# Early gate projections, early products with D, the first states' transfers on ScalarE's queue, and another PSUM room for the value product, in a one-core AdaLN layer

## The chip, the cores and the metric

One core of a Trainium2 chip runs the whole program in one launch. The metric is the device time in microseconds (us) of one execution. TensorE is PE in the views, VectorE is DVE, ScalarE is ACT, GpSimd is POOL and SyncE, which here only issues DMAs, is SP.

## The reference

```python
h = layernorm(x) * (1 + ca) + sa               # x: 4 batches, 2048 tokens, 512 columns, f32
x = x + ga * attn(h)
h = layernorm(x) * (1 + cb) + sb
x = x + gb * ffn(h)

attn(u):   omega = clip(softplus(u W_omega^T + b)); zeta = sigmoid(u W_zeta^T + b); F = u W_B^T + b_B
           A = omega^2; S = 1/(1 + DT^2 A); d = 1 - zeta      # 64 oscillators, states z and y
           z, y = d (S z - DT A S y), d (DT S z + S y)        # a scan over the 2048 tokens
           z, y = z + F[:64], y + F[64:]
           return [z y] C^T + u D_mat^T
ffn(x):    x_prev = x shifted by one token
           r = sigmoid((mu_r x + (1 - mu_r) x_prev) W_r^T)
           k = (mu_k x + (1 - mu_k) x_prev) W_k^T
           return r * (relu(k)^2 W_v^T)
```

sa, ca, ga, sb, cb and gb are six rows for each batch, made from a small input by one product with `wmod`; ga and gb are kept at least 0.25 away from zero.

## The kernel before

The tokens are cut into 8 blocks of 256, and each block has 4 batches, so there are 32 units; unit i is block s = i // 4, batch b = i % 4. Each unit passes through two classes. `gts[i]` (a gate unit) makes the inputs of the scan: `project` multiplies the transposed, not yet normalized x (`xt`, loaded transposed from DRAM) with a weight that holds (1 + ca) already (`wgb`, L233); `norm` finds the layernorm's factors on ScalarE (L185, L191) and POOL (L195 to L197); `send` writes these factors as rows to DRAM (`st`, L201), and `spread` reads them back to all partitions (`bc`, L212); `multiply` applies them to the projection (L251), and `deliver` sorts the result into the block's `maps` with its bias (L264, L266). When all four gate units of a block are delivered, `scan(s)` runs the recurrence on VectorE: softplus and damping, 8 steps inside each of 32 chunks (L306 to L319), a tree over the chunks up and down (L335 to L353), and the states at the end (L374 to L381). `by_batch` sorts the states (ScalarE L401 for block 0, VectorE L404 for the others), and eight DMAs carry them to `y` (L407). The scan of the next block runs beside the finish units of this one: its pieces wait in a list `side`, and `take(budget)` puts as many of them into VectorE's order as the budget, in us, allows.

`fin[i]` (a finish unit) does the rest. In block 0: `attend` makes the product with D (`direct`, L463, into PSUM `pd_c`) and the product of the states with C (`states`, L486, into `pc_c`), and VectorE adds both to x (L471, L513); then come the second layernorm (`normalize`, ScalarE L573), `mix` (transposes on PE, L593; scaling and token shift in turn on ScalarE L599 and VectorE L602, the first column on POOL L605), `key` (L626, relu and square on ScalarE L630, L617), `receptance` (L738, L740) and `value` (L753, then L756, L757 and the store). The loop runs one unit ahead: in stage i it does the key of unit i, `attend` of unit i+1, the receptance of i, the `mix` of i+1, the value of i. From block 1 on key and receptance are made by another method with seven products in place of eight, and D and C go into one PSUM sum.

D_mat is different for each batch (scaled by ca and ga), so a `Turn` job for each batch makes it: `d_scaled` scales rows on VectorE (L958) with a row that PE has spread over the partitions (`scale_rows`, L122), `rows` scales with ga on ScalarE (L972), `turn` transposes on PE (L981), `keep` copies back on ScalarE (L985), and `keep_in_dram` saves it (L795), because its SBUF room `dg` serves other things later.

All instructions of an engine run in the order in which the program text issues them, DMA issues included: there is no scheduler here. POOL and ScalarE issue DMAs out of the same order as their arithmetic, so a DMA that has to wait holds what stands behind it. A DMA also waits for the one that had its completion semaphore before it (eight are used in turn by all DMAs of SP and ScalarE).

In block 0 before the change the order was: projections of units 0 to 3, scan(0) in one piece on VectorE, the six rows of wmod, D for batches 0 and 1, products with D of units 0 and 1, projections 4 and 5, then the states; D for batches 2 and 3, the products with D of units 2 and 3, and the projections 6 to 9 stood behind the states, between the stages of the loop.

Of the kernel before, what the change touches and what calls it, by code (L numbers as in the profile page):

```python
# [9 lines left out]
F32 = mybir.dt.float32  # L10
# [11 lines left out]
P = 128  # L22
# [28 lines left out]
def adaln_layer_kernel(ctx: ExitStack, tc: tile.TileContext, x, x_t, c_t, wmod, w_gate, w_b, b_gate, b_f, c_mat, d_mat,  # L51
# [76 lines left out]

    y_of = {}

    class Block:
# [15 lines left out]
    class Gates:  # L147
# [89 lines left out]
        def project_pieces(self):  # L237
            u = self.u

            def piece(i, k):  # L240
                if i == k == 0:
                    self.pg = ps1.tile([P, 2, W], F32, tag="pg", name=f"pg_{u.tag}")
                nc.tensor.matmul(  # L243
                    self.pg[:, i, :], wgb[:, u.b, k, ts(i, P)], self.xt[:, k, :], start=(k == 0), stop=(k == KC - 1)
                )

            return [lambda i=i, k=k: piece(i, k) for i in range(2) for k in range(KC)]

        def multiply(self, tag="g"):
# [18 lines left out]
    def scan(s):  # L268
# [123 lines left out]
        def by_batch(q):  # L392
# [12 lines left out]
            for r in range(2):  # L405
                for i in range(2):
                    nc.sync.dma_start(y_of[s][ts(i, M), 2 * q + r, :], t[i][ts(r, M), :])  # L407

# [16 lines left out]
    class Finish:  # L425
# [46 lines left out]

        def products(self, room=(ps3, "px")):

            self.pd = [self.direct(n, room) for n in range(NT)]

        def add_products(self):
            for n in range(NT):
                self.add_direct(n, self.pd[n])

        pd = None

# [5 lines left out]
        def attend(self, between):  # L488
# [11 lines left out]

            if self.pd is not None:
                for n in range(NT):
                    states_apart(n)
            for n in range(NT):
                if self.pd is None:
                    pd = self.direct(n, stop=not self.fast)
                    if self.fast:
                        self.states(n, pd, False)
                    else:
                        states_apart(n)  # L510
                    self.add_direct(n, pd)
                if not self.fast:
                    nc.vector.tensor_add(self.x[:, n, :], self.x[:, n, :], pcs[n])  # L513
                if n == 0:
                    self.stats(n)
                    between()
# [225 lines left out]

        def value(self, between, parts=1):

            act, xt, u = self.act, self.x, self.u
            n_col = D // parts
            for n in range(NT):
                r = self.r[n]
                for h in range(parts):
                    at = ts(h, n_col)  # L750
                    pv = ps2.tile([P, D], F32, tag="pm", name=f"pv_{self.tag}_{n}_{h}")[:, :n_col]
                    for j, k in enumerate(range(KC) if parts == 1 else (2, 3, 0, 1)):
# [137 lines left out]
    gts[3].xt = p1.tile([P, KC, W], F32, tag="act", name="xt_3")  # L890
    load_transposed(gts[3].u, gts[3].xt)
    weights_to(dn, d_mat, nc.sync)
    weights_to(dt, d_t, nc.sync)
    wm_ga = wmod_to(wvb[:, 2], 2)

# [66 lines left out]
    class Turn:  # L962


        def __init__(self, b):
            self.dst, self.b = dg[:, b], b
            self.room = (ps2, "pm") if b < 2 else (ps3, "px")

# [5 lines left out]
        def turn(self):  # L974
            self.pts = [
                pool.tile([P, D], F32, tag=tag, name=f"turn_d{self.b}_{k}")
                for k, (pool, tag) in enumerate([(ps2, "pt")] * 2 + [self.room] * 2)
            ]
# [4 lines left out]
        def keep(self):  # L983
            for k in (2, 3, 0, 1) if self.b < 2 else range(KC):
                nc.scalar.copy(self.dst[:, k, :], self.pts[k])  # L985

    c_rows = dg[:, 3]

    def c_scaled(b, n):
        nc.vector.tensor_mul(cg[:, b : b + n], cn.unsqueeze(1).broadcast_to([P, n, D]), c_rows[:, b : b + n])  # L990

# [18 lines left out]
    def shift_rows():  # L1010

        nc.sync.dma_start(col_rows.rearrange("i b d -> (i b) d"), rows3)
        nc.sync.dma_start(c_rows, col_rows[2:3].broadcast_to([P, B, D]))
        for i in range(2):
            fin[i].shift_row = fin[i].row(0)
        fin[0].gate_row = fin[0].row(1)
# [51 lines left out]
    gts[3].multiply("soft")  # L1068
    gts[3].deliver(share=1)
    pcas = [scale_rows(b) for b in range(2)]  # L1070
    side += scan(0)
    take(0.1)
    take(0.1)
    for b in range(2):
        d_scaled(b, pcas[b])
    gts[4].load()
    weights_to(wk, w_k, nc.sync)
    weights_to(wn, w_v, nc.sync)
    take(100)

    pr = rows_of(all_mod, dt, D, "mean")
    rowm = p2.tile([P, D], F32, tag="r", name="row_mean")
    nc.scalar.copy(rowm, pr)
    rowa = mod_rows(wm_ga, "ga")
    wm_sb = wmod_to(wvb[:, 2], 3)
    nc.scalar.copy(pmean, turned(rowm, "mean", 2 * B))
# [4 lines left out]
    turn_d = [Turn(b) for b in range(B)]  # L1093
    xs67 = p1.tile([P, 4, D], F32, tag="mixed", name="xs67")
    gts[4].norm()
    gts[4].send(nc.gpsimd)
    rowb = mod_rows(wm_gb, "gb", room=px)
    turn_d[0].rows()
    rowc = mod_rows(wm_cb, "cb", room=px)
    gts[5].load()  # L1100
    xt45 = wvb[:, 1].rearrange("p k d -> p (k d)").rearrange("p (i k w) -> p i k w", i=2, k=KC)
    for i in (4, 5):
        gts[i].xt = xt45[:, i - 4]
        load_transposed(gts[i].u, gts[i].xt)
    for i in (6, 7):
        gts[i].xs = [xs67[:, NT * (i - 6) + n, :] for n in range(NT)]
        load_natural(gts[i].u, xs67[:, NT * (i - 6) : NT * (i - 5), :])
    gate_cols(gb, turned(rowb, "gb"), "b")
    nc.scalar.activation(mod[:, CB], turned(rowc, "cb"), AF.Identity, bias=1.0)
    pr = ps2.tile([P, D], F32, tag="pt", name="pd0row")  # L1110
    for e in range(KC):
        nc.tensor.transpose(pr[: 3 * B, ts(e, P)], cols[:, e].rearrange("p i b -> p (i b)"), ident)
    nc.scalar.copy(rows3, pr[: 3 * B, :])
    shift_rows()
    turn_d[0].turn()
    turn_d[0].keep()
    keep_in_dram("dg", 0)
    row = mod_rows(wm_sb, "sb", room=px)
    xt67 = wvb[:, 2].rearrange("p k d -> p (k d)").rearrange("p (i k w) -> p i k w", i=2, k=KC)
    for i in (6, 7):  # L1120
        gts[i].xt = xt67[:, i - 6]
        load_transposed(gts[i].u, gts[i].xt)
    gts[4].spread(nc.gpsimd)
    turn_d[1].rows()
    nc.scalar.copy(mod[:, SB], turned(row, "sb"))
    shift_factors()
    gts[5].norm()
    gts[5].send(nc.gpsimd)
    fin[0].products()
    turn_d[1].turn()  # L1130
    turn_d[1].keep()
    keep_in_dram("dg", 1)
    gts[4].project()
    pcas = [scale_rows(b, pm) for b in range(2, B)]
    gts[5].spread(nc.gpsimd)
    fin[1].products((ps2, "pt"))
    gts[5].project(ps3.tile([P, 2, W], F32, tag="px", name="pg_5"))


    c_scaled(0, 2)  # L1140
    take(1)
    fin[0].add_products()
    fin[0].shift(nc.vector)
    fin[1].add_products()
    gts[4].multiply()
    gts[6].norm()
    gts[6].send(nc.gpsimd)
    fin[0].attend(lambda: None)
    fin[0].normalize()
    c_scaled(2, 2)  # L1150
    d_scaled(2, pcas[0])
    d_scaled(3, pcas[1])
    gts[6].project()
    fin[1].shift(nc.vector)
    weights_to(wr, w_r, nc.sync)
    gts[7].norm()
    gts[7].send(nc.gpsimd)
    gts[6].spread(nc.gpsimd)
    fin[0].mix(lambda: None)
    gts[7].project(ps3.tile([P, 2, W], F32, tag="px", name="pg_7"))  # L1160
    gts[8].load_t()
    gts[4].deliver(share=1)
    gts[5].multiply()
    gts[5].deliver(share=1)
    gts[7].spread(nc.gpsimd)
    gts[8].load()
# [5 lines left out]
    def gates(j):  # L1172
        gts[j].project()
        gts[j].multiply()
        gts[j].deliver()

    def turn(*jobs):
        for t in jobs:
            t.turn()
            t.keep()  # L1180

    def rows(*jobs):
        for t in jobs:
            t.rows()

# [6 lines left out]
    for i, f in enumerate(fin):  # L1192
        at = i % B
        ahead = fin[i + 1] if i + 1 < len(fin) else None
        if i < 4:
# [5 lines left out]
            if i == 0:  # L1201
                ahead.attend(lambda: None)
                ahead.stats(NT - 1)
                ahead.norm_factors()
            if i < 2:
                rows(turn_d[i + 2])
            if i == 0:
# [9 lines left out]
            if i == 3:  # L1217
                sums_t(receptance_weights, quarters_of(wr))
            if i:
                ahead.attend(lambda: take(2))  # L1220
                ahead.normalize()
            else:
                ahead.norm_apply()
            value_scaled(i)
            if i == 3:
                fetch("dg", i + 3)
            if i == 0:
                gts[7].multiply()
                gts[7].deliver(share=1)
                gts[8].norm_dve()  # L1230
                gts[8].send()
                gts[8].spread()
                gts[9].norm_dve()
                gts[9].send()
            if i == 1:
                gates(9)
            if i:
# [3 lines left out]
            if i == 0:  # L1241
                side += scan(1)
                take(0.1)
                take(0.1)
            gts[i + 9].load_t()
            gts[i + 9].spread()
            f.value(lambda: take(3 if i == 0 else 4))
            if i < 3:
                ahead.gate_row = ahead.row(1)
            if i < 2:  # L1250
                turn(turn_d[i + 2])
                keep_in_dram("dg", i + 2)
                gates(8 if i == 0 else 10)
        else:
# [181 lines left out]
```

## Time and profile before

| what | value |
|---|---|
| times of three runs | 1139.86, 1146.07, 1148.36 us (median 1146.07) |
| profiled execution | 1144.09 us, of which the span of the instructions is 1142.3 us |
| granted TensorE clock over the span | 0.981 of full speed |
| PE busy | 1092.9 us (96%) |
| DVE busy | 756.1 us (66%) |
| ACT busy | 646.9 us (57%) |
| POOL busy | 185.0 us (16%) |
| moved by DMA | 177.73 MB, 156 GB/s on average |
| first product with states (`pc_c`) | starts at 102.00 us |
| first product of block 1 with D (`pd_c` at L463) | starts at 244.06 us |

Times inside the profile are us from the start of the span. "Idle before" is the time for which an engine stood still ahead of an instruction, and the arrow names what ended it. A matmul in f32 is shown as two instructions, so "x16" is eight matmuls.

### The profile page before, as it was taken

Reading aid. Unit: us, or ns where it says so; the run is one execution under the profiler, and the core shown is the slowest. Engines: PE = TensorE matmul, PEld = TensorE weight load, DVE = VectorE, ACT = ScalarE, POOL = GpSimd, SP = SyncE. Lnnn points to the kernel's source line nnn. Section 1 sums busy time; section 2 is a strip of 40 time slices with the busy share of each in tenths; the row PEclk is TensorE's granted clock in tenths of the full one; section 3 lists DMA queues with packets and bytes.
Section 4 is the critical chain, followed back from the end, with each engine's and each line's share of the span. In section 5 each row is a group of like instructions: output and inputs, shape, how many; then the busy total and the mean of one; then the engine's idle time right before and its main releaser. Section 6 shows DMA issues by size and latency. Waiting matters only on the chain.

```text
span 1142.3 us, 14439 instructions
## 1 busy us (share of the span) xinstructions
PE 1092.9 (96%) x4692; PEld 732.8 (64%) x4692; DVE 756.1 (66%) x1838; ACT 646.9 (57%) x1336; POOL 185.0 (16%) x377
## 2 busy tenths in 40 slices
PE   7895898989999999999999999999999999999998
PEld 4553464556667667766666677666666665566666
DVE  5793776746876568666876568665876567664444
ACT  1651764535666576557666576557665565434443
POOL 1221211121122111111111111111121101111110
PEclk9888998999999999999999999999999999999999
DMA  9985569346056754474556854474565644444211
GB/s 312 298 138 111 143 135 202 104 126 217 24 178 191 193 162 161 141 173 130 166 178 188 187 171 127 146 200 119 178 176 170 162 139 138 148 157 138 102 56 37
DMA packets 138803, 177.73 MB, mean 156 GB/s; under 512 B 22876, under 2 KB 96860, under 8 KB 130920
## 3 DMA queue, kind: packets, MB, share of 16 engines
q1 hardware_dynamic: 135720, 175.49, 54.4%
q10 hardware_dynamic: 2688, 0.79, 0.3%
q0 software_dynamic: 320, 0.53, 0.3%
q8 instruction: 37, 0.61, 0.2%
q14 instruction: 38, 0.31, 0.1%
HBM read 147.34 MB, written 25.25 MB: 151 GB/s over the span
## 4 chain that ended last, share of the span: by engine, by line
PE 69%; DMA 14%; DVE 7%; ACT 6%; issue 1%; SPq 1%; POOL 1%; DVEq 0%; POOLq 0%; ACTq 0%
PE pv_c L753 14%; PE pd_c L531 13%; PE pxk_c L656 7%; DMA xt<-in_x_t_dram 7%; PE pxr_c L656 7%; PE pg L243 5%; PE pzk_c L656 4%; DMA bc<-st 3%; PE pzr_c L656 3%; PE pd_c L486 3%; PE pg L233 2%; PE pk_c L626 2%; PE pr_c L738 2%; PE pt_c L593 2%; PE pyk_c L656 2%; PE pyr_c L656 2%
## 5 line engine op out<-in xcount | busy, mean ns | idle before, releaser
L753 PE MATMUL pv_c<-wvb,act_c 128*128 128x512 f32 (+1 forms) x528 | 226.6, 582 | 4.5 <-ACT r_c L740 4.5
L531 PE MATMUL pd_c<-dg,xt 128*128 128x512 f32 x432 | 206.2, 593 | 0.0
L753 PEld LDWEIGHTS pv_c<-wvb,act_c 128*128 128x128 f32 x528 | 100.0, 191 | 111.4 <-issue 100.3
L602 DVE SCALAR_TENSOR_TENSOR mixed_c<-pt_c,prev_f,mixed_c 128x255 f32<-128x255 f32 x256 | 118.1, 481 | 72.3 <-ACT mixed_c L599 72.1
L599 ACT ACTIVATE mixed_c<-pt_c,mod,now_f 128x256 f32<-128x256 f32 x256 | 130.2, 559 | 25.3 <-DVE mixed_c L602 19.5
L266 ACT ACTIVATE maps<-g,bias 64x256 f32<-64x256 f32 x112 | 83.1, 742 | 73.4 <-DVE g L251 65.9
L531 PEld LDWEIGHTS pd_c<-dg,xt 128*128 128x128 f32 x432 | 74.5, 191 | 55.9 <-issue 54.3
L243 PE MATMUL pg<-xt,wgb 128*128 128x256 f32 x320 | 85.4, 379 | 0.0
L471 DVE SCALAR_TENSOR_TENSOR x<-pd_c,rs,x 128x512 f32<-128x512 f32 x64 | 47.6, 746 | 52.5 <-PE pd_c L486 49.6
L550 ACT ACTIVATE xn_c<-x 128x512 f32<-128x512 f32 x44 | 27.7, 629 | 94.0 <-DVE x L471 89.8
L656 PEld LDWEIGHTS pxk_c<-dg 128*128 128x128 f32 x448 | 58.6, 191 | 27.0 <-issue 23.9
L573 ACT ACTIVATE xn_c<-x,mean_c,var_c 128x512 f32<-128x512 f32 x64 | 48.6, 808 | 42.1 <-POOL mean_c L569 42.0
L456 POOL TENSOR_TENSOR x<-x,row 128x1024 f32<-128x1024 f32 x30 | 70.9, 2363 | 8.5 <-DMA row<-col_rows 8.5
L243 PEld LDWEIGHTS pg<-xt,wgb 128*128 128x128 f32 x320 | 59.2, 190 | 7.2
L656 PE MATMUL pxk_c<-dg 128*128 128x128 f32 x448 | 59.1, 275 | 0.7 <-ACT act_c L665 0.7
L486 PE MATMUL pd_c<-cg,y 128*128 128x512 f32 x112 | 56.3, 593 | 0.0
L656 PE MATMUL pxr_c<-wvb 128*128 128x256 f32 x208 | 53.4, 379 | 0.0
L756 DVE TENSOR_TENSOR r_c<-pv_c,r_c 128x512 f32<-128x512 f32 (+1 forms) x66 | 44.0, 667 | 9.2 <-PE pv_c L753 9.2
L605 POOL TENSOR_TENSOR mixed_c<-mixed_c,edge_c 128x4 f32<-128x4 f32 x64 | 12.8, 201 | 215.1 <-ACT mixed_c L599 200.9
L251 DVE TENSOR_TENSOR g<-pg,bc 128x512 f32<-128x512 f32 x32 | 22.0, 687 | 38.7 <-DMA bc<-st 20.2
L757 DVE TENSOR_TENSOR r_c<-r_c,x 128x512 f32<-128x512 f32 (+1 forms) x66 | 44.6, 676 | 2.3
L674 DVE TENSOR_TENSOR act_c<-act_c,pzk_c 128x256 f32<-128x256 f32 x28 | 11.7, 419 | 51.8 <-PE pzk_c L656 51.8
(245 smaller groups left out, 2023.3 us busy)
## 6 DMA issues: line engine op xcount, KB each, us to landing
dg<-dg SPq DMA_DIRECT2D x30, 1024.0 KB, 7.0
xt<-in_x_t_dram SPq DMA_DIRECT2D x116, 256.0 KB, 7.8
wvb<-wv SPq DMA_DIRECT2D x26, 1024.0 KB, 15.0
x<-in_x_dram SPq DMA_DIRECT2D x32, 512.0 KB, 7.0
out_dram<-r_c SPq DMA_DIRECT2D x62, 256.0 KB, 2.1
xs<-in_x_dram SPq DMA_DIRECT2D x54, 256.0 KB, 12.2
row<-col_rows SPq DMA_DIRECT2D x36, 256.0 KB, 16.5
wvb<-in_wmod_dram SPq DMA_DIRECT2D x5, 1024.0 KB, 8.9
```

Source lines behind the costliest of these rows:

```text
L243: nc.tensor.matmul(self.pg[:, i, :], wgb[:, u.b, k, ts(i, P)], self.xt[:, k, :], start=(k == 0), stop=(k == KC - 1))
L266: nc.scalar.activation(there, here, AF.Identity, scale=sign, bias=bias[src, i, b : b + 1])
L456: engine.tensor_tensor(xt, xt, self.shift_row.unsqueeze(1).broadcast_to([P, NT, D]), ALU.add)
L471: nc.vector.scalar_tensor_tensor(xt, pd, r, xt, ALU.mult, ALU.add)
L486: nc.tensor.matmul(pc, y_of[u.s][:, u.b, ts(n, P)], cg[:, u.b, :], start=start, stop=True)
L531: nc.tensor.matmul(pds[n], self.h[:, k, ts(n, P)], dg[:, self.at, k, :], start=(k == 0), stop=False)
L573: nc.scalar.activation(self.xn[:, n, :], self.x[:, n, :], AF.Identity, bias=self.mean[:, n : n + 1], scale=self.var[:, n : n + 1],)
L599: nc.scalar.activation(m, pt, AF.Identity, bias=mod[:, SB, k, b : b + 1], scale=now_f[:, b, i, k : k + 1])
L602: nc.vector.scalar_tensor_tensor(m[:, 1:], pt[:, : W - 1], prev_f[:, b, i, k : k + 1], m[:, 1:], ALU.mult, ALU.add)
L656: nc.tensor.matmul(to[:, j, :], left[:, k, ts(j, P)], right[:, k, :], start=start and j == k == 0, stop=(k == 1), skip_group_check=True,)
L753: nc.tensor.matmul(pv, act[:, k, ts(n, P)], wvb[:, self.at, k, at], start=(j == 0), stop=(j == KC - 1))
L757: nc.vector.tensor_add(r[:, at], r[:, at], xt[:, n, at])
```

## The change

Names and lines in the diff are those of the program text. What it does:

- The transposed x of gate units 4 to 7 is loaded early into the rooms of `dg[2]` and `dg[3]`, and their projections are made before the states. Each result is copied out of PSUM by ScalarE (`keep_raw`), to be multiplied later. Projections 8 and 9 stand directly after the first products with states, where 6 and 7 stood, and are kept in the same way.
- All four `Turn` jobs and the products with D of finish units 0 to 3 stand before the states. ScalarE scales each product by the layernorm's factor on its way out of PSUM (`products`), and VectorE adds the two tiles of a unit in one instruction (`add_products`). `d_scaled` for batches 2 and 3 stands inside scan(0), after its reciprocals and after its third chunk step.
- `by_batch` of block 0 issues the transfers of the states on ScalarE's queue.
- C's rows come in two halves, the second one after the room of the first early product is free.
- `norm` of units 8 and 9 is on ScalarE; it was `norm_dve` on VectorE. The norms of units 6 and 7 read x from `wr`, and W_r is loaded when both are done.
- `value` of units 0 to 3 takes its PSUM from the pool `px` (three rooms) in place of `pm` (two rooms, which receptance uses too).

```diff
+    raw_gates = wvb[:, 1].rearrange("p k d -> p (k d)").rearrange("p (g i w) -> p g i w", g=4, i=2)
+    made_early = [wvb[:, b // 2 * 2, ts(b % 2, NT), :] for b in range(B)]
...
+        def keep_raw(self):
+            raw = raw_gates[:, self.u.i % 4]
+            nc.scalar.copy(raw, self.pg)
+            self.pg = raw
...
-                    nc.sync.dma_start(y_of[s][ts(i, M), 2 * q + r, :], t[i][ts(r, M), :])
+                    (nc.sync if s else nc.scalar).dma_start(y_of[s][ts(i, M), 2 * q + r, :], t[i][ts(r, M), :])
...
-            self.pd = [self.direct(n, room) for n in range(NT)]
+            for n in range(NT):
+                r = rs[:, self.u.b, self.u.s, 0, n : n + 1]
+                nc.scalar.activation(made_early[self.u.b][:, n, :], self.direct(n), AF.Identity, scale=r)
         def add_products(self):
-            for n in range(NT):
-                self.add_direct(n, self.pd[n])
+            nc.vector.tensor_add(self.x, self.x, made_early[self.u.b])
...
-        def value(self, between, parts=1):
+        def value(self, between, parts=1, room=(ps2, "pm")):
...
+    rowa = mod_rows(wm_ga, "ga")
+    wm_sb = wmod_to(wvb[:, 2], 3)
+    pr = rows_of(all_mod, dt, D, "mean")
...
     for b in range(2):
         d_scaled(b, pcas[b])
+    gts[4].project()
...
+    take(6.3)
...
     rowb = mod_rows(wm_gb, "gb", room=px)
+    rowc = mod_rows(wm_cb, "cb", room=px)
+    gts[4].keep_raw()
+    gts[5].project(ps3.tile([P, 2, W], F32, tag="px", name="pg_5"))
+    gts[4].norm_means()
     turn_d[0].rows()
...
+    gts[5].keep_raw()
...
+    gts[6].project()
+    turn_d[0].turn()
+    turn_d[0].keep()
+    pca = scale_rows(2)
+    d_scaled(2, pca)
+    take(6)
+    turn_d[1].rows()
+    row = mod_rows(wm_sb, "sb", room=px)
+    gts[6].keep_raw()
...
+    gts[4].norm_squares()
+    gts[4].send(nc.gpsimd)
+    gts[7].project()
     fin[0].products()
     turn_d[1].turn()
     turn_d[1].keep()
+    gts[7].keep_raw()
+    pca = scale_rows(3)
+    d_scaled(3, pca)
+    take(100)
+    turn_d[2].rows()
...
+    fin[1].products()
+    turn_d[2].turn()
+    turn_d[2].keep()
+    gts[8].load_t()
+    gts[5].norm()
+    gts[5].send(nc.gpsimd)
+    turn_d[3].rows()
+    fin[2].products()
+    turn_d[3].turn()
+    turn_d[3].keep()
     gts[5].spread(nc.gpsimd)
+    gts[9].load_t()
+    fin[3].products()
     take(1)
+    c_scaled(0, c01)
     fin[0].add_products()
     fin[0].shift(nc.vector)
     fin[1].add_products()
+    c23 = c_rows(2, made_early[0])
     gts[4].multiply()
     gts[6].norm()
     gts[6].send(nc.gpsimd)
     fin[0].attend(lambda: None)
     fin[0].normalize()
...
+    gts[8].project()
+    gts[4].deliver(share=1)
+    gts[8].keep_raw()
     fin[1].shift(nc.vector)
+    gts[6].spread(nc.gpsimd)
+    fin[0].mix(lambda: None)
+    gts[9].project(ps3.tile([P, 2, W], F32, tag="px", name="pg_9"))
     gts[7].norm()
     gts[7].send(nc.gpsimd)
+    weights_to(wr, w_r, nc.sync)
...
             if i:
+                if not ahead.fast:
+                    ahead.add_products()
                 ahead.attend(lambda: take(2))
...
-                gts[8].norm_dve()
+                gts[8].norm()
...
-                gts[9].norm_dve()
+                gts[9].norm()
...
-            f.value(lambda: take(3 if i == 0 else 4))
+            f.value(lambda: take(3 if i == 0 else 4), room=px)
...
-            if i < 2:
-                turn(turn_d[i + 2])
-                keep_in_dram("dg", i + 2)
-                gates(8 if i == 0 else 10)
+            if i == 0:
+                gts[8].multiply()
+                gts[8].deliver()
+            if i == 1:
+                gates(10)
```

## Prediction

> **What bounds the kernel now.** I read the granted clock and the tenths first, then the busy times of three stretches, PE's order of time, the chain that ended last, and POOL's order of time.
>
> ```profile
> PE   7895898989999999999999999999999999999998
> DVE  5793776746876568666876568665876567664444
> PEclk9888998999999999999999999999999999999999
> ...
> 39.00:102.00 63.00, 44.81 (x191) 26.05 (x189) 44.28 (x102) 28.44 (x62) 14.00 (x41) 0.84 0.88 182
> 102.00:244.00 142.00, 126.84 (x432) 81.20 (x433) 97.69 (x213) 79.50 (x145) 23.31 (x40) 0.94 0.58 141
> 244.00:1142.00 898.00, 890.34 (x3930) 603.15 (x3928) 592.40 (x1455) 529.10 (x1114) 143.45 (x282) 1.00 0.51 148
> ```
>
> The columns of the last three lines are the length, then the busy us of PE, PE's weight loads, DVE, ACT and POOL, the clock, the DMA share and GB/s. From 244 us on PE is full (890 of 898), and the change does not touch that part. So the change is worth the shift of one moment: the first product with D of block 1, at 244.06 now. Before it there are two stretches. From 39 to 102 us block 0's scan sets the end; from 102 to 244 PE is 89% busy.
>
> ```profile
> 86.78 3.62 PE L233 MATMUL pg<-wvb,wgb 128*128 128x256 f32 x16
> 102.00 3.75 PE L486 MATMUL pc_c<-cg,y 128*128 128x512 f32 x4 [11.60 <-DMA y<-maps]
> ...
> 137.16 8.54 PE L753 MATMUL pv_c<-wvb,act_c 128*128 128x512 f32 x16 [2.87 <-ACT r_c L740]
> ...
> 179.19 7.13 PE L753 MATMUL pv_c<-wvb,act_c 128*128 128x512 f32 x16 [1.60 <-ACT r_c L740]
> ...
> 231.94 8.83 PE L626 MATMUL pk_c<-mixed_c,wk 128*128 128x256 f32 x32 [3.12 <-DVE r_c L756]
> ```
>
> PE stands 11.6 us for the states. A wait of about 3 us also costs the clock: the product after it takes 8.83 in place of 7.07 us, while 1.60 us costs nothing (7.13 against 7.03).
>
> ```profile
> 80.94 2.07 ACT maps L401 x4
> ...
> 85.55 2.06 SPq L795
> ...
> 88.33 13.58 DMA y<-maps
> 101.91 0.09 issue
> 102.00 3.77 PE pc_c L486 x4
> ...
> 115.74 0.82 POOL L201 DMA_DIRECT2D st<-rs  x1 [0.29 <-POOL rs L197]
> 116.57 0.56 POOL L212 DMA_DIRECT2D bc<-st  x1
> 117.12 0.20 POOL L583 COPY edge_c<-first_f 128x8 f32<-128x8 f32 x1
> 117.41 0.20 POOL L605 TENSOR_TENSOR mixed_c<-mixed_c,edge_c 128x4 f32<-128x4 f32 x1
> ...
> 127.64 0.59 POOL L212 DMA_DIRECT2D bc<-st  x1 [9.02 <-DVE mv_c L127]
> 129.18 0.72 POOL L568 TENSOR_TENSOR var_c<-var_c,neg_half 128x2 f32<-128x2 f32 x1 [0.95 <-DVE mean_c L565]
> ```
>
> The states were sorted at 83.0 and usable at 102.0: the transfers stood on SP behind a save of D, then 13.6 us in the queue. The POOL lines show a hidden wait: `bc` (L212) stands in POOL's order and reads what `st` (L201) wrote, so POOL stands until `st` has landed. The view of DMA landings gives POOL's four `st` 10.0, 13.6, 14.1 and 11.3 us, though each moves only 2 KB. What stands behind `bc` on POOL is the column that key needs (L605) and the layernorm factors (L568).
>
> **What leaves the part after the states.** Two projections (3.45 each), the D products of units 2 and 3 (6.87 each) and two turns (1.75 each): 24.1 us of PE. It comes back only where PE sets the end.
>
> **The part before the states.** I place the built program's order and waits with the durations above. PE is free of projection 3 at 39.1. It makes two row products (0.9 each), two spread rows (0.9), projection 4, columns and rows (3.7), projection 5, columns (1.9) and projection 6: 58.6. Turn 0 ends at 60.4, and the spread row for D of batch 2 at 61.3. Now ScalarE copies turn 0 (2.05), scales D 1 (2.85), copies a row and projection 6 (1.05): 66.4, and projection 7 waits for that last copy, PE idle 3.4 us, so with 1.7 us for the clock it ends at 71.5. D products 0 end at 78.4, turn 1 at 80.2. From here PE and ScalarE alternate: turn, 1.55 us until the third of four copies is out, 6.87 of products, 1.75 of turn. With 0.95 for a column product, products 1 end at 89.6, products 2 at 99.8, products 3 at 110.0. ScalarE scales the last one (0.65), sorts half of the states (two copies, 1.04), and issues two transfers (0.55 each): 112.8.
>
> DVE loses more, unseen: `d_scaled` for batch 2 stands after the reciprocals (52.9) and waits for its row until 61.3; that for batch 3 stands from 70.0 until PE's row at 81.1, and each takes 2.25. After it 22.0 us of scan remain (58.24 to 81.4 now, less 1.1 for C): the scan ends at 105.3, 24 us later, but 5 us ahead of ScalarE.
>
> On ScalarE's queue nothing stands before the transfers that has not landed: y's other blocks land in 2.0 us (median; the bounds are 1.9 and 12.1), so states at 114.8, against 102.0. I take 2.0, since the saves of D are done by then. The Trainium skill's page "DMA: Bandwidth & Descriptors", section "Issuing engines are not separate DMA queues", speaks against any gain here: DMAs of all engines run on the same 16 DMA engines, and another issuing engine saves the issue time alone. By it block 0's own 11.5 us would stand and the states come at 124.3; the row of the later blocks says that the queue's contents made the delay. Clock losses after the three waits of 1.55 us: 0 to 1.7 each, taken as 0.
>
> **After the states, T = 114.8.** Norm 6 now stands behind the transfers on ScalarE and ends at T+5; its `st` is issued at T+7. `bc` 6 and then key's first column stand behind its landing. With 11.3 us, 0.6 for `bc` and two small steps, key 0 starts at T+20 (now T+15.7; PE waits 5.5 and loses 1.8), receptance 0 ends at T+37.4. Norm 7 ends at T+19.5, `st` 7 is issued at T+22, and `bc` 7 holds POOL until T+34.5, with unit 1's factors behind it: xn 1 at T+36.2 (now T+29.3). W_r is loaded from T+19.5; a megabyte lands in 4.8 us alone (C's rows) and 14.1 loaded, and receptance 0 needs it at T+30.5: 0 to 3 us, taken as 0.
>
> Then ScalarE is the path. Gate 7 waits for `bc` 7's landing (4.0 to 6.7) and is delivered by T+43.2. Norms 8 and 9 follow (8 passes, 5.5), with 1.3 us for the fourth x tile, whose room norm 8 frees (release to use took 2.65 at 135.4); table load and sigmoids 2.4; half of mix 1 2.9. Key 1 starts at T+55.4, now T+48.7, with 24 us less on PE. Scan(1)'s functions begin after mix 1 and end at T+62.1 (now T+45.9). The value room gives back the 2.87 us wait at 137.16, but PE then waits longer for mix 1.
>
> From T+62.1 DVE is full up to unit 3's second add: scan(1) 34.5, mix 2 4.5, unit 2's adds and statistics 4.6, unit 3's adds 2.6, three output pairs 4.1, three gates 2.1, scaled W_v 2.35, key sums 2.6: 57.4, so T+119.5. Then statistics and factors 3.4, xn and transposes 2.2, value 2 with a clock loss 8.7, key 3 6.9, projection 11 3.45: T+144.2, or 259.0 against 244.06. That is 14.9 us later.
>
> Costed at nothing: norms 8 and 9 leave DVE (3.5 us) while it idles; one add for two (0.3 a unit); copies of projections 8 and 9 stand in ScalarE's gaps around key 0; C's second half lands before norm 6. Transposed x for projection 10 lands in 7.8 (median) to 17.7 us: if the latter, DVE's third gate is up to 7 us late.
>
> The profiled execution of before is 1144.09 for a span of 1142.3; the median of the runs is 2.0 above it. I add the shift to the median: 1161.0.
>
> **The rivals.** First, POOL's wait is covered (`st` lands in a few us, or the mix is late anyway): key 0 at T+16, scan(1) from T+54.2, the end at T+136.3, 251.1: 7.0 later, 1153.1. For it: `st` on a quieter queue; against: 10.0 us was the least of four. Second, the states come no sooner on ScalarE's queue: with 12.1 us T is 124.9, 25.0 later in all, 1171. For it: the save of D 3 and x for unit 9 are in flight at 104 to 110; against: nothing large is in flight at 112. Third, on the other side: PE, not ScalarE and DVE, is the bound behind the states. Its 89% there speak for it. Then the 24.1 us return in full and the value waits (2.87, 1.60, 3.12) go too: 12.8 - 24.1 - 7.6 is 18.9 us earlier, 1127. It decides if key 1 starts before about T+36. Against it: DVE's 97.7 and ScalarE's 79.5 us there stay, in an order with longer waits.
>
> **How the numbers follow.** Forecast 0.52, first rival 0.25, second 0.13, third 0.10. A change of 1% is 11.5 us, about what a measurement here tells from none. Slower by over 1%: the second rival and most of the forecast, 0.62; within 1%: most of the first and the forecast's lower edge, 0.29; faster 0.09. The forecast's own range (`st` 10.0 to 14.1, clock losses 0 to 5, x 10 late by 0 to 7) is 1154 to 1171; with the first and second rivals it is 1147 to 1174.
>
> **What would show it.** Right: `pc_c` of unit 0 at 112 to 118; DVE idle about 8 and 11 us at `d_scaled`; key 0 released by POOL's L605 form; scan(1) starting 60 us or more after `pc_c`; PE idle over 5 us before key 1. Wrong: `pc_c` before 106, or PE over 85% busy between `pc_c` and block 1.

## The result, and the profile after

The changed kernel takes 1159.4 us in the median of four runs (1158.4 to 1161.1), the kernel before 1146.6; the ratio is 1.0124 (95% interval 1.0082 to 1.0167). The prediction was 1161.0. The profiled execution of the changed kernel has a span of 1157.3 us, against 1142.3.

The kernel before does not take the same time everywhere. In the four series of runs of this case, not all on one chip, its medians were 1146.6, 1144.2, 1125.5 and 1140.1 us. So every kernel below is compared within its own series, with the kernel before or with a neighbour that ran beside it.

The tenths and the granted clock of the page after:

```profile
PE   7987867889999999999999999999999999999998
...
PEclk8999888889999999999999999999999999999999
```

PE's fourth to ninth slices are 7 8 6 7 8 8, where they were 5 8 9 8 9 8, and the clock of the fifth to ninth is 8 throughout, where it was 9 9 8 9 9. The three stretches, cut at the first product with states and at the first product of block 1 with D (length, then busy us of PE, weight loads, DVE, ACT, POOL, then clock, DMA share, GB/s):

```profile
39.00:117.25 78.25, 63.94 (x284) 39.17 (x273) 47.81 (x102) 43.61 (x83) 12.68 (x37) 0.96 0.63 191
117.25:259.80 142.55, 109.73 (x336) 68.42 (x337) 89.26 (x199) 79.07 (x155) 25.28 (x46) 0.88 0.41 109
259.80:1157.30 897.50, 889.93 (x3929) 603.32 (x3927) 592.75 (x1455) 529.22 (x1114) 144.35 (x282) 1.00 0.52 149
```

The last stretch is what it was (897.5 us, 898.2 before). It is not quite a constant: in the profiles of all runs it takes 895.0 (e6) to 901.8 us (e2), so a difference of a few us between two times need not lie ahead of block 1. The states come 15.25 us later. The stretch behind them has 17.1 us less busy time on PE (109.73 against 126.84; the work moved away was 24.1 at full clock, and what is left runs at a clock of 0.88 in place of 0.94), and yet it is as long as before (142.55, before 142.06 to the same product): PE is busy 77% of it in place of 89%. PE's order of time shows both parts:

```profile
92.73 7.13 PE L470 MATMUL pd_c<-dg,xt 128*128 128x512 f32 x16 [1.60 <-ACT dg L992]
99.70 1.91 PE L988 MATMUL turn_d<-ident,dg 128*128 128x128 f32 x16
103.21 7.13 PE L470 MATMUL pd_c<-dg,xt 128*128 128x512 f32 x16 [1.60 <-ACT dg L992]
117.25 3.75 PE L492 MATMUL pc_c<-cg,y 128*128 128x512 f32 x4 [6.91 <-DMA y<-maps]
...
132.19 7.17 PE L629 MATMUL pk_c<-mixed_c,wk 128*128 128x256 f32 x32 [1.08 <-POOL mixed_c L608]
...
168.69 9.25 PE L629 MATMUL pk_c<-mixed_c,wk 128*128 128x256 f32 x32 [6.29 <-POOL mixed_c L608]
...
185.77 9.20 PE L741 MATMUL pr_c<-wr,mixed_c 128*128 128x512 f32 x16 [6.11 <-ACT act_c L633]
...
211.24 6.69 PE L235 MATMUL pg<-xt,wgb 128*128 128x256 f32 x16 [5.65 <-DMA xt<-in_x_t_dram]
```

From projection 7 (65.74, after a wait of 3.47 us) to 110.3 PE waits at most 1.6 us per unit, each time for ScalarE's copy of a turn, and the products themselves push the states back. Behind the states the short waits of before have become waits of 4 to 6 us, and the product after each takes up to 9.25 us where it takes 7.07 at full clock. The chain of waits names what stands in them:

```profile
110.97 1.10 ACT maps L408 x2
112.07 0.08 ACTq L414
112.25 4.87 DMA y<-maps
117.25 3.77 PE pc_c L492 x4
...
137.18 12.41 DMA st<-rs
150.17 4.12 DMA bc<-st
154.38 0.70 DVE g L258
...
158.67 2.64 DMA xs<-in_x_dram
...
165.12 1.09 ACT r_c L743 x2
```

The `st` of unit 7, 2 KB, is the largest piece of that chain between the states and block 1; `bc` stands behind its landing, gate 7 behind `bc`, the norms of units 8 and 9 behind gate 7 on ScalarE (156.60 to 163.8, with 1.7 us of it for an x tile), and then the sigmoids and `mix` of unit 1. POOL's order of time shows what else stood there:

```profile
131.06 0.59 POOL L214 DMA_DIRECT2D bc<-st  x1 [6.00 <-DMA st<-rs]
131.64 0.20 POOL L586 COPY edge_c<-first_f 128x8 f32<-128x8 f32 x1
131.93 0.20 POOL L608 TENSOR_TENSOR mixed_c<-mixed_c,edge_c 128x4 f32<-128x4 f32 x1
...
150.17 0.55 POOL L214 DMA_DIRECT2D bc<-st  x1 [12.14 <-DMA st<-rs]
150.74 0.72 POOL L571 TENSOR_TENSOR var_c<-var_c,neg_half 128x2 f32<-128x2 f32 x1
```

POOL stands 6.0 and 12.1 us in the issue of `bc`, with key's first column and then the layernorm factors of unit 1 behind it.

A third moment splits the stretch behind the states: the end of the logarithm of scan(1) on ScalarE (147.84 before, 175.46 after), from which VectorE can run the next scan. It is used for all kernels below. The start of its line, before and after:

```profile
147.21 0.63 ACT L285 ACTIVATE soft<-soft 128x512 f32<-128x512 f32 x1
...
174.83 0.63 ACT L292 ACTIVATE soft<-soft 128x512 f32<-128x512 f32 x1
```

| us | states at | states to logarithm | logarithm to block 1 | block 1 at |
|---|---|---|---|---|
| before | 102.00 | 45.84 | 96.22 | 244.06 |
| after | 117.25 | 58.21 | 84.34 | 259.80 |
| change | +15.25 | +12.37 | -11.88 | +15.74 |

So 11.9 us came back behind the logarithm (e8 below tells what they seem to be), and the two earlier parts spent them and 15.7 us more.

### The profile page after: what moved, and what is told of

Its sections match the earlier page's. It is cut to its first block, busy times and chain, and to the rows that moved or that the text cites. A ratio compares the mean times of both kernels' runs of the same rounds, so it can differ in the third digit from the quotient of the medians.

```text
span 1157.3 us, 14456 instructions
## 1 busy us (share of the span) xinstructions
PE 1094.4 (95%) x4692; PEld 733.2 (63%) x4692; DVE 752.1 (65%) x1824; ACT 661.4 (57%) x1366; POOL 186.6 (16%) x379
## 4 chain that ended last, share of the span: by engine, by line
PE 72%; DMA 12%; ACT 7%; DVE 5%; SPq 2%; issue 1%; POOL 1%; ACTq 0%; DVEq 0%; POOLq 0%
PE pv_c L756 15%; PE pd_c L534 12%; PE pxk_c L659 7%; PE pxr_c L659 6%; PE pg L245 5%; DMA xt<-in_x_t_dram 4%; DMA bc<-st 4%; PE pg L235 4%; PE pzk_c L659 4%; PE pzr_c L659 3%; PE pd_c L492 3%; PE pd_c L470 3%; DMA st<-rs 2%; PE pt_c L596 2%; PE pr_c L741 2%; PE pyk_c L659 2%
## 5 line engine op out<-in xcount | busy, mean ns | idle before, releaser
L659 PEld LDWEIGHTS pxk_c<-dg 128*128 128x128 f32 x448 | 58.7, 191 | 26.1 <-issue 24.1
L478 DVE SCALAR_TENSOR_TENSOR x<-pd_c,rs,x 128x512 f32<-128x512 f32 x56 | 41.7, 745 | 48.5 <-PE pd_c L492 48.4
L741 PE MATMUL pr_c<-wr,mixed_c 128*128 128x512 f32 x96 | 44.4, 618 | 6.5 <-ACT act_c L633 6.1
L596 PE MATMUL pt_c<-ident,xn_c 128*128 128x128 f32 x256 | 36.1, 284 | 13.3 <-ACT xn_c L576 13.3
## 6 DMA issues: line engine op xcount, KB each, us to landing
xs<-in_x_dram SPq DMA_DIRECT2D x54, 256.0 KB, 12.4
```

The lines of the kernel that those rows point to most:

```text
L596: nc.tensor.transpose(pt[:, j, ts(n, P)], xn[:, n, ts(2 * g + j, P)], ident)
L659: nc.tensor.matmul(to[:, j, :], left[:, k, ts(j, P)], right[:, k, :], start=start and j == k == 0, stop=(k == 1), skip_group_check=True,)
L741: nc.tensor.matmul(pr, mixed[:, 0, k, ts(n, P)], wr[:, k, :], start=(k == 0), stop=(k == KC - 1))
```

## The experiments

Theory: the states are later because turns and D products now stand ahead of them on PE and ScalarE, and the part behind is set by POOL's stand at `bc` and by ScalarE's norms, not by PE. Rivals: VectorE's stops inside scan(0) make the states late; the queue of the transfers does; PE is the bound behind the states.

### e1: the states' queue alone, in the kernel before

```diff
-                    nc.sync.dma_start(y_of[s][ts(i, M), 2 * q + r, :], t[i][ts(r, M), :])
+                    (nc.sync if s else nc.scalar).dma_start(y_of[s][ts(i, M), 2 * q + r, :], t[i][ts(r, M), :])
```

> The kernel before, with one edit of the change alone: the eight transfers of block 0's states go on ScalarE's queue. My theory: it was SP's queue that made the states late (sorted at 83.0 us, usable at 102.0). ScalarE has nothing ahead of them, so they land 2 to 5 us after their issue, PE reaches `pc_c` straight from projection 5 at 90.5 to 92.5, and the rest, whose length hangs on its own chains, shifts by the same 10 us: 1136 us (1133 to 1140). Rival (the issuing queue is of no account, since all DMAs share the same engines): `pc_c` at 98 to 102, 1143 to 1147 us.

1137.0 us against 1144.2; ratio 0.9956 (0.9923 to 0.9988). `pc_c` starts at 91.40, as expected. The transfers land in 4.7 to 7.2 us, against 10.5 to 12.1 in the profile of before. But block 1 starts at 236.91, only 7.2 us earlier than in the profile of before. The chain of waits shows where the rest went:

```profile
78.23 16.60 DMA dg<-dg
94.85 0.47 ACTq L407
95.37 0.77 ACT xs L185 x3
```

The last issue on ScalarE waits until the save of D for batch 1, issued on SP, has landed. It is the eighth DMA of the two engines behind that save, so the kernel's rule that eight completion semaphores are used in turn by all DMAs of SP and ScalarE would make it so. Norm 6, at 82.8 before, starts at 95.4, and unit 0's factors stand behind its factors on POOL. So the edit alone is a gain in the kernel before, less than `pc_c` gained, since ScalarE now stands in its own issues.

### e2: the changed kernel with the states on SP

```diff
-                    (nc.sync if s else nc.scalar).dma_start(y_of[s][ts(i, M), 2 * q + r, :], t[i][ts(r, M), :])
+                    nc.sync.dma_start(y_of[s][ts(i, M), 2 * q + r, :], t[i][ts(r, M), :])
```

> The changed kernel with the transfers of block 0's states back on SP's queue. Ahead of them on SP stand only the save of D 3 (issued at 103.7) and the x of unit 9 (104.1 to 106.1). Theory that the contents of SP's queue decide: these are through by 112, so the states land nearly as soon and the time is that of the changed kernel, 1158 to 1161. Theory that SP's queue is slow by itself: the 13.6 us of before come back in place of 4.9, `pc_c` at about 126 and 1168 us.

1160.0 us, as expected of the first theory; the ratio to before is 1.0177 (1.0118 to 1.0236). `pc_c` is at 115.58, block 1 at 256.11; the transfers land in 1.9 to 2.0 us on SP, against 2.2 to 4.5 on ScalarE's queue. With the states this late, their queue is of no account. The changed kernel itself was not run in this series, and e2 stands for it there; that the two take the same time rests on the other series (1159.4 and 1159.3).

### e3: norms of units 8 and 9 on VectorE

```diff
-                gts[8].norm()
+                gts[8].norm_dve()
...
-                gts[9].norm()
+                gts[9].norm_dve()
```

> The changed kernel with the norms of units 8 and 9 back on VectorE. My theory (ScalarE's order is the path from gate 7 to mix 1): the 7.2 us that they take on ScalarE between gate 7 (156.6) and the sigmoid's table (163.8) go, VectorE makes them in its idle 156 to 167; key 1 and scan(1) start 6 to 7 us earlier: 1153 us (1151 to 1156). Rival (VectorE's work sets the end of the stretch): 3.5 us more on VectorE, 1159 to 1163. Rival (PE or its waits for other things): 1159.

1154.0 us, 6.0 less than e2 beside it. From the states to the logarithm it takes 50.05 us (56.80 in e2, 58.21 in the changed kernel), and from the logarithm to block 1 85.87 (83.73 in e2). ScalarE's missing work gives 6.8 us ahead of the logarithm, and behind it 2.1 are lost, where VectorE has the extra work. Key 1 no longer waits:

```profile
161.23 7.07 PE L629 MATMUL pk_c<-mixed_c,wk 128*128 128x256 f32 x32
```

Up to the logarithm ScalarE's order was the path. The 6.0 us are not all of that kind: e3 keeps the states on ScalarE's queue, they come 1.9 us later than in e2 (117.44), and block 1 starts 2.75 us earlier (253.36). In the two profiled executions the rest lies behind block 1 (897.5 against 901.8 us), where the edit changes nothing.

### e4 and e6: factors of units 6 and 7 ahead of the states

```diff
+    gts[6].norm()
+    gts[6].send(nc.gpsimd)
     gts[5].spread(nc.gpsimd)
     gts[9].load_t()
-    fin[3].products()
+    fin[3].products(gts[7].norm)
+    gts[7].send(nc.gpsimd)
...
-    gts[6].norm()
-    gts[6].send(nc.gpsimd)
...
-    gts[7].norm()
-    gts[7].send(nc.gpsimd)
     weights_to(wr, w_r, nc.sync)
```

`products` calls its argument between its two tiles.

> The changed kernel with the norms of units 6 and 7 and their `st` moved ahead of the states, into ScalarE's idle time at 103.6 and 107.6; nothing else is moved. My theory (`bc` on POOL waits for `st` and holds key's first column and unit 1's factors): key 0 starts about 2 us earlier against the states, unit 1's factors 7 to 8 us earlier (at states + 27 in place of + 34), gate 7 is delivered 9 us earlier, and norms 8 and 9, mix 1 and scan(1) follow: 1150.5 us (1147 to 1154). Rival (POOL's wait is covered by VectorE or PE): 1158 to 1160.

1166.6 us, slower by 6.6 than e2 beside it: a miss. The stretch behind the states did become shorter (136.20 us; logarithm after 52.86), but the states came at 128.69. The chain of waits, and SP's own order:

```profile
110.97 17.62 DMA y<-maps
```

```profile
109.01 0.39 SPq L822 DMA_DIRECT2D wr<-in_w_r_dram  x1
111.36 14.71 SPq L160 DMA_DIRECT2D xs<-in_x_dram  x3
```

The earlier norms had freed the room of W_r. Its load (1 MB) and three x tiles went out in the same microseconds as the states. e6 is e4 with the states on SP, so that these loads stand behind them in the same order.

> As e4_factors_early, but the states' transfers go on SP's queue, ahead of the loads of W_r and of x for units 8 and 9. In e4 these loads, freed by the earlier norms, were issued at 109.0 and 111.4, ahead of the states, and a transfer of the states took 17.6 us in place of 4.9: `pc_c` at 128.7. My theory (the early factors shorten the stretch, the collision undid it): `pc_c` at 114 to 117, the stretch behind it as long as in e4 (136.2 us), 1150 to 1154 us. Rival (the collision is not the cause, or the loads collide with `st` and the gates instead): 1159 or more.

1148.3 us, 6.1 less than e5 beside it (told next; it has the changed kernel's states and its order behind them, and differs from e6 in the queue of the states and in the scan as well). From the states to the logarithm 51.20 us (56.40 in e5), and the stretch is 132.85 long. `pc_c` only came at 118.15, since the states took 7.2 to 10.2 us to land; with W_r behind them that is not W_r. What shared the time with them there (the `st` of units 6 and 7, `bc` of unit 5, the save of D 3) was not tried apart. POOL no longer stands for a landing:

```profile
135.34 0.77 POOL L214 DMA_DIRECT2D bc<-st  x1 [1.26 <-DVE g L258]
143.47 1.15 POOL L573 TENSOR_TENSOR var_c<-var_c,neg_half 128x2 f32<-128x2 f32 x1 [7.36 <-DVE mean_c L570]
```

Unit 1's factors now start when VectorE has its statistics. That `bc` held them in the changed kernel is shown: with the factors early, the part from the states to the logarithm takes 52.86 us in e4 and 51.20 in e6, without them 56.4 to 58.2 (changed kernel, e2, e5, e9). That the loads made e4's loss is what the rows and the order say, and e6 mends most of it.

### e5: scan(0) in one piece

```diff
-    pca = scale_rows(2)
-    d_scaled(2, pca)
     take(6)
...
-    pca = scale_rows(3)
-    d_scaled(3, pca)
+    pcas = [scale_rows(b) for b in (2, 3)]
     take(100)
+    d_scaled(2, pcas[0])
+    d_scaled(3, pcas[1])
```

> The changed kernel with `d_scaled` of batches 2 and 3 (and their spread rows) moved behind the whole of scan(0), so that VectorE no longer stands 8.4 and 11.2 us inside the scan. My theory (the alternation of turns, copies and D products on PE and ScalarE sets the moment of the states, VectorE has 5 us to spare): the scan ends near 82 us in place of 103, and still `pc_c` stays at 115 to 119 and the time at 1157 to 1162 us. Rival (VectorE's two stops delay the states): `pc_c` comes 10 to 19 us earlier and the time falls to 1141 to 1150.

1154.4 us, 2.6 below the range expected; ratio to before 1.0253 (1.0218 to 1.0288) in a series in which before takes 1125.5. The changed kernel was not run beside it, so the time alone does not tell what the edit is worth; the moment of the states does. In VectorE's order of time the scan's last big addition (L384) ends at 79.65, where it ended at 103.4 in the changed kernel, and nothing follows from it:

```profile
78.42 1.23 DVE L384 TENSOR_TENSOR maps<-maps 128x1024 f32<-128x1024 f32 x1
82.29 4.49 DVE L966 SCALAR_TENSOR_TENSOR dg<-pca,wr 128x2048 f32<-128x2048 f32 x2 [2.65 <-PE pca L122]
```

```profile
118.77 3.75 PE L492 MATMUL pc_c<-cg,y 128*128 128x512 f32 x4 [6.79 <-DMA y<-maps]
```

`pc_c` starts no sooner. A scan whose last big addition ends 24 us sooner does not bring the states while their sorting stands on ScalarE behind the last D product. The rival of VectorE's stops is out.

### e7 and e8: two pieces in the kernel before

```diff
-    keep_in_dram("dg", 1)
     gts[4].project()
...
     take(1)
+    keep_in_dram("dg", 1)
```

> The kernel before, with only the save of D for batch 1 moved behind the states' eight transfers in SP's order; they stay on SP. Theory that the transfer ahead in SP's queue made the states late, and that e1 lost part of its gain because ScalarE stood in its own DMA issues until 95.4: the states land by 90 to 92, norm 6 keeps its early place on ScalarE, the whole shift of 10 to 11 us comes through: 1134 us (1132 to 1137). Rival (other transfers on the same engines, the transposed x of units 6 and 7 above all, hold the states as well): `pc_c` at 96 or later, 1138 to 1144.

1121.3 us against 1125.5; ratio 0.9957 (0.9930 to 0.9985). The gain is there, its theory is not: `pc_c` is at 98.28, in a profile in which the same place of e8, with the save still ahead, is at 99.32. The issue of the transposed x for units 6 and 7 held SP until 83.7, and the states took 5.8 to 9.7 us to land. The rival fits this profile; but the profiled execution is the slowest of its ten (1127.55), so what brought the 4.3 us is open, and in e12 below the same edit had `pc_c` at 93.29.

```diff
-            f.value(lambda: take(3 if i == 0 else 4))
+            f.value(lambda: take(3 if i == 0 else 4), room=px)
```

> The kernel before, with only the other PSUM room for the value products of units 0 to 3. The waits of 2.87 and 1.60 us ahead of two value products, and the clock lost after the first, go: value 0 at 134.3 in place of 137.2, key 1 near 147 in place of 150.7. Theory that chains on ScalarE and VectorE set the length behind the states: the gain is taken back at the next waits (x for projection 10, key 3), 1142 to 1146 us. Rival (PE is the bound there): 4 to 6 us, 1138 to 1141.

1124.2 us against 1125.5; ratio 0.9981 (0.9960 to 1.0003). The waits ahead of two value products are gone, two others of 2.5 and 2.8 us stand ahead of the turns (for VectorE's `carry`), and the time does not tell it from no change. Its profile has one more use. In its part from the logarithm to block 1 (84.47 us) PE is busy 81.08, at full clock; in the changed kernel that part is 84.34 us long with PE busy 65.03. Of e8 and of the changed kernel:

```profile
144.98:229.45 84.47, 81.08 (x286) 51.37 (x285) 64.06 (x148) 47.37 (x92) 12.36 (x19) 1.00 0.65 161
...
175.46:259.80 84.34, 65.03 (x196) 39.76 (x195) 63.56 (x146) 40.73 (x80) 11.76 (x19) 0.88 0.52 132
```

So where x comes in time, the moved PE work bought 3 us at most even there (the part is 82.54 long in e5 and 81.65 in e6, beside e8 in one series). The 96.22 us of the profile of before hold the wait for x of projection 10 (4.02), its clock loss and the wait of key 3; e12 below, with a wait of 5.85 us for that x, takes 93.14. The part from the logarithm to block 1 is 81.7 to 85.9 us in every variant of the changed kernel.

### e9 to e12: the changed kernel again, an order with the states sooner, and the pieces of before

e9 is the changed kernel itself.

> The changed kernel itself, once more, beside the kernel before on one chip. The kernel before took 1146 us with its own profile and 1125 us in the call of e5 to e8, where its transfers landed sooner; the changed kernel with an unbroken scan (e5) took 1154 there. Theory (the changed kernel's start is set by an alternation of PE and ScalarE and by ScalarE's and POOL's order behind the states, not by large transfers): `pc_c` at 116 to 119, the first product of block 1 at 256 to 260 and 1155 to 1161 us, wherever the kernel before stands. Rival (both gain alike from sooner transfers): 1137 to 1145 where the kernel before takes 1125.

1159.3 us; ratio 1.0164 (1.0127 to 1.0200) with before at 1140.1. `pc_c` at 117.56, block 1 at 256.78. In three series the changed kernel (or e2 for it) took 1159.3 to 1160.0, while the kernel before moved from 1140.1 to 1146.6. So the same change costs 12.8, 15.9 (e2) or 19.2 us, by the series. In the series where before took 1125.5 the changed kernel itself was not run, so the rival of e9 was not put to its test; e5, at 1154.4 there, speaks against it.

e10 keeps all the moved work and changes the order; the states go on SP, as in e2 (the main lines of its edit):

```diff
     take(100)
+    take(1)
+    keep_in_dram("dg", 1)
+    d_scaled(2, pcas[0])
+    d_scaled(3, pcas[1])
     turn_d[2].rows()
...
     fin[2].products()
+    fin[0].attend(lambda: None)
     turn_d[3].turn()
     turn_d[3].keep()
...
     fin[3].products()
+    gts[6].norm()
+    gts[6].send(nc.gpsimd)
+    fin[0].mix(lambda: None)
+    gts[8].project()
```

> The changed kernel with the order of one stretch changed: scan(0) is unbroken as in e5, the states are sorted and sent (on SP, ahead of the save of D for batch 1) right after it, and the first products with states stand ahead of turn 3 and the D products of unit 3; transposes of unit 0 ahead of projection 8. No work is removed. My theory (the D products that stand ahead of the states set their moment, and the stretch behind hangs on it): `pc_c` at 101 to 104 in place of 117, key 0 at 121 to 125 in place of 132, key 1 9 to 11 us earlier, and the time 8 to 11 us under that of e9. Rival (the order of PE does not matter, something behind the states sets the end): within 3 us of e9.

1151.8 us, 7.5 less than e9, half a us short of the range expected; ratio to before 1.0098 (1.0067 to 1.0128).

```profile
99.65 1.88 PE L494 MATMUL pc_c<-cg,y 128*128 128x512 f32 x4
```

`pc_c` is 17.9 us earlier and no longer waits, so the order ahead of it made the states late; what the unbroken scan and each moved product have in it was not tried apart. Key 0 is at 119.63, but key 1 at 159.68 (7.8 earlier) and the logarithm only 66.80 us after the states. POOL took the rest, as the chain of waits shows:

```profile
117.02 11.92 DMA st<-rs
...
131.72 9.93 DMA st<-rs
142.23 3.33 DMA bc<-st
```

Norm 7's factors on POOL stand behind `bc` 6, which waits for `st` 6; then `bc` 7 waits for `st` 7: two landings in a row.

e11 is e10 with e3, and with norms and `st` of units 6 and 7 on either side of turn 3:

```diff
     fin[0].attend(lambda: None)
+    gts[6].norm()
+    gts[6].send(nc.gpsimd)
     turn_d[3].turn()
...
+    gts[7].norm()
+    gts[7].send(nc.gpsimd)
     fin[3].products()
-    gts[6].norm()
-    gts[6].send(nc.gpsimd)
...
-                gts[8].norm()
+                gts[8].norm_dve()
```

> e10 with the two other cures: norms of units 8 and 9 on VectorE (e3: 5.4 us) and norms and `st` of units 6 and 7 ahead of `mix` of unit 0 (e6: about 6 us against e5). If the three lie on one path one after another, they add: 18 to 24 us under e9, 1134 to 1141 us. Rival (behind the first cure VectorE's full stretch from scan(1) on is the bound, or x for later units): 10 to 14 us under e9.

1147.1 us, 12.2 less than e9; ratio 1.0052 (1.0029 to 1.0074). The gains do not add, as the rival said. The logarithm is done at 163.20, and 84.85 us follow, but the transposed x of unit 9 now stands in PE's way:

```profile
126.57 5.42 PE L235 MATMUL pg<-xt,wgb 128*128 128x256 f32 x16 [8.19 <-DMA xt<-in_x_t_dram]
```

It took 17.57 us to land, issued with the save of D 3, W_r and three x tiles. The profiled execution is the slowest of its twelve (1151.05), so the wait may be shorter in the others.

e12 is e7 and e8 together, the kernel before with two edits.

> The kernel before with the two pieces that helped alone: the save of D for batch 1 behind the states' transfers (e7: ratio 0.9957) and the other PSUM room for value (e8: 0.9981). If they add: ratio 0.992 to 0.996 to the kernel before, 5 to 9 us. Rival (the room gives nothing once the states come sooner): 0.995 to 0.998.

1132.6 us against 1140.1; ratio 0.9927 (0.9894 to 0.9959). That fits two pieces that add (0.9957 times 0.9981 is 0.9938), but the interval also holds the upper edge of the rival's gain (0.995), so what the room adds is not shown. It is the lowest ratio of all versions, with none of the moved PE work, though its interval overlaps those of e1 and e7.

## Why the prediction was right

The direction, the size (12.8 us forecast as 14.9) and the steps held. The size is less certain than that: with the kernel before of the other series the change costs 15.9 (e2) or 19.2 us (e9), and that the forecast lies among them is in part luck, since it did not know how much the kernel before moves. Point by point, by the names of its steps (T is the start of `pc_c`):

- The part before the states. The last D product was to end at 110.0 and ends at 110.34. PE's wait for the copy of projection 6 was 3.4 and is 3.47; the stops at `d_scaled` were to be about 8 and 11 us:

```profile
60.78 2.29 DVE L966 SCALAR_TENSOR_TENSOR dg<-pca,wr 128x2048 f32<-128x2048 f32 x1 [8.35 <-PE pca L122]
...
80.66 2.29 DVE L966 SCALAR_TENSOR_TENSOR dg<-pca,wr 128x2048 f32<-128x2048 f32 x1 [11.23 <-PE pca L122]
```

 That they do not delay the states, since ScalarE was later still, e5 shows.
- T. 114.8 against 117.25. The term that was too small is the transfer: 2.0 us, taken from the other blocks, where the chain has 4.87. It lies inside the bounds given (1.9 and 12.1; the upper one was not of other blocks but of block 0's own transfers in the kernel before). The second rival, with 12.1, is out: the eight landed in 2.2 to 4.5 us.
- Key 0 was to start at T+20 and starts at T+14.9. Norm 6 ended at T+2.8, not T+5, and `st` landed in 9.3 us, not 11.3. POOL's column was its releaser, as said, with 1.1 us of wait in place of 5.5.
- The factors of unit 1 and gate 7. `xn` was to come at T+36.2 and came at T+34.5; gate 7 was to be delivered by T+43.2 and was at T+39.3, since `bc` 7 went out at T+32.9, not T+34.5, and landed in 4.1 us. (The bounds of 4.0 to 6.7 for this landing left out one of the four of before, 10.8.)
- ScalarE's path. Norms 8 and 9 with the x tile 6.8 us (7.2); key 1 at T+55.4 (T+51.4); scan(1)'s functions done at T+62.1 (T+58.2, so the mark of 60 us was missed by 2). The 4 us are gate 7's.
- VectorE's full stretch: 57.4 us to unit 3's second add (58.6), and 24.7 to block 1 (25.8). The end, 259.0, against 259.80. VectorE is full there as forecast (busy 52.6 of 58.5 us). But a second path is level with it, which the prediction had named only as a possible delay of VectorE's third gate: the chain of waits goes by the x of projection 10 (10.67 us to land, 5.65 us of wait on PE), and both reach unit 3's normalization at 237.4. Which of them sets the end was not tried apart. An excess of 2.5 us in T, a shortfall of 3.9 behind it and 2.3 us more at the end nearly cancel; that the end is right to a microsecond is luck.
- The first rival (POOL's wait is covered) is refuted by e4 and e6, whose part up to the logarithm is 3.5 to 7 us shorter with the factors early. The third (PE is the bound behind the states) is refuted by the windows above (PE is at 77%) and by key 1 at T+51.4, where it needed T+36; e3 also gains without touching PE's work.

On the rule of the Trainium skill's page "DMA: Bandwidth & Descriptors", section "Issuing engines are not separate DMA queues", the runs are divided. For it: e2, where the queue makes no difference, and e4, where a transfer of ScalarE's queue took 17.6 us beside loads issued on SP. It allows for a gain in issue time alone, and calls that usually small. In the kernel before it is not small: on SP the save holds the queue for 4.74 us and the eight issues take 14.30. In e1 the states were used 10.6 us sooner than in the profile of before, and the time fell by 7.2 us beside it. Part of this is the place in the issue order; but the transfers also landed in a median of 6.0 us in place of 11.5, and since the two profiles are of two series (in e8, with SP's order as before, the median was 8.4), how much of that the queue made stays open.

## What to carry to other kernels

Work that is moved ahead of the point that releases a long serial chain is not free because it must be done anyway: here it moved the states by 15 us, while PE had waits behind them to do it in. Split such a stretch at its releases (states, logarithm, next block) and ask of each part which engine sets it. PE at 89% looked like the bound; with its work moved away the first part grew by 12.4 us, and the second was at most 3 us shorter than in e8, the kernel before with the x of projection 10 in time. And before a DMA that must land is given a place in an engine's order, look at what stands behind it on that engine, and at which loads an earlier step sets free beside it.

## What was not expected of the hardware

- A DMA issued by ScalarE stood until a DMA of SP had landed (e1: the save of D, 16.6 us after its issue), and held ScalarE's arithmetic for 5.5 us; the transfers themselves landed in at most 7.2 us. A completion semaphore that both share fits this, as told at e1.
- Four DMA issues on ScalarE take 2.45 us, and its copy of the next half came 2.06 us late for them; in e1 the same four took 6.30.
- The kernel before took 1125.5 to 1146.6 us in four series; in the fast one e8 had no wait for the x of projection 10, which cost the profile of before 4.0 us and a slow product. The changed kernel (e2 for it in one) moved by 0.7 us over three of the series; it was not run in the fast one. That the landing of transfers makes all of this difference was not tried apart. The 2 KB of `st` took 8.7 us (unit 6 in e5) and 12.4 (unit 7 in the changed kernel).
